# Attention outputs stored undivided, divided in the last unit and in the projection; row maxima made behind the values of a step

## The chip, the cores and the metric

The kernel runs on one core of a Trainium2 chip. The metric is the device time of one execution, in microseconds. A core has five engines that run side by side, each through its own instruction stream in order: TensorE (PE: matmuls; PEld is its weight load), VectorE (DVE), ScalarE (ACT), GpSimd (POOL) and SyncE (SP, which here only issues DMAs). Matmuls write to banks of PSUM; everything else lives in SBUF or in DRAM.

## The reference

One transformer block with conditioning, for `x` of 2 batches x 2048 tokens x 512 features, 16 heads of width 32:

```python
mod = silu(condition) @ Wada + bada
sh_a, sc_a, gt_a, sh_m, sc_m, gt_m = split(mod, 6)
xm = layernorm(x, g1, be1) * (1 + sc_a) + sh_a
q, k, v = split_heads(xm @ Wqkv)
attn = softmax(where(causal, q @ k.T / sqrt(32), -inf))
x = x + gt_a * ((attn @ v) @ Wproj + bproj)
xm = layernorm(x, g2, be2) * (1 + sc_m) + sh_m
x = x + gt_m * (gelu(xm @ W1 + b1) @ W2 + b2)
```

What the change is about is the division inside the softmax: `attn @ v` is the sum of `exp(score - max) * v` over the keys, divided by the sum of `exp(score - max)`.

## The kernel before

The program runs five stages one after the other: QKV of batch 0 (`Qkv.run`), attention of batch 0 (`attention_phase`), projection of batch 0 (`project_phase`) with QKV of batch 1 behind it, attention of batch 1, and projection of batch 1 with the MLP of both batches behind it.

**Units and steps.** Attention is cut into 16 units per batch. Unit `u` is a pair `(c, i)`: `c` is a chunk of four heads (128 features) and `i` a block of 512 queries (`QB`). The list is `units`: for `c` = 0 the blocks come as 0, 1, 2, 3, for `c` = 1, 2, 3 as 0, 2, 1, 3. A unit has `4i + 3` steps, each over one tile of 128 keys (`steps_of`): 3, 7, 11 or 15 steps. The four last units (12 to 15) belong to `c` = 3; their blocks are `last_order` = 0, 2, 1, 3, and the last unit is block 3 with 15 steps.

**A step.** `scores_t` puts on PE, for each of the four heads, a matmul that lays minus the row maxima into a bank (`st<-fold,sel`), then the scores with keys on the partitions on top of it (`st<-qst,kst`). ACT makes `e` = exp of the bank; on the diagonal POOL clears what is masked (`affine_select`). Two steps later (`LAG` = 2) PE multiplies `e` with the values into the PSUM bank `o` (`values`) and with ones into the bank `sm` (`row_sums`; off the diagonal POOL first adds two steps' `e` into `ee`, so that one matmul serves two steps). These late matmuls wait in the list `pending` and are put on PE by `flush(now)`, after the step's scores.

**The maxima.** The maxima must be known before a unit starts, so its scores are computed a first time with queries on the partitions: `Row.score` puts those matmuls (`s<-kst,qst`) in between those of a step, up to two units ahead (`AHEAD`), at a pace that `due` works out. They go into the pool `ps_s`, which has two banks (one in a step may borrow an `st` bank instead). DVE reads each bank once for its maximum (`mx<-s`, line 363; with the causal mask, line 358) and so frees it. When a unit's maxima are complete, `split` makes two small copies (`mhl`) and `Row.rows` transposes them on PE into a bank of `ps_s` (`ps_m`) and spreads them on DVE into `fold`, one `fold` for even and one for odd units. In a step of `attention_phase`, `row.rows(u + 1)` stands between the scores and `flush(now)`.

**The end of a unit.** `finish` copies `o` and `sm` to SBUF on ACT (`ot`, `sums`). Then SP, DVE, SP, SP, DVE and SP take turns: a DMA spreads the sums over the partitions (`r<-sums`), DVE inverts them (line 532), a DMA writes them to DRAM (`r<-r`), a DMA reads them back, each row spread over 32 partitions (`rb<-r`), DVE multiplies (`ot<-ot,rb`, line 540), and a DMA stores the block (`o<-ot`) to `od[b][i][:, c, :]`.

**Projection.** `project_phase` takes the blocks in the order of `last_order`, four tiles of 128 tokens each: PE multiplies the loaded block (`at`) with `wproj` in four matmuls, DVE adds `x` (to which POOL has added `bgate`) and takes the statistics for the next norm. `wproj` and `bgate` are `Wproj` and `bproj` times the gate; `gate_weights` makes them in the QKV stage of the batch, with one matmul (`ps_rows`) and five DVE products. `Row.prefetch`, called in the last unit's step 3, loads the first two blocks (`at_s`), the first tokens (`xt_s`) and the next stage's first tokens (`next_s`) into the space of the keys `kst0`, which are no longer needed by then.

**Order.** PE's matmuls and ACT's exps and copies stay in the order in which the code issues them (`tc.keep_in_program_order`). What goes to DVE, POOL and the DMA queues is put in order by the framework's scheduler when the program is built; on the chip each engine then takes its stream strictly in that order, and waits at the first instruction that isn't ready. Tiles of one tag share a ring of `bufs` buffers: `qst` (the queries of a unit, 4 buffers), `kst0`, `e`, `ee`, and the PSUM banks.

Of the kernel before, what the change touches and what calls it, by code (L numbers as in the profile page):

```python
# [27 lines left out]
def dit_block_kernel(  # L28
# [94 lines left out]
    for r in (0, HD):  # L123
# [19 lines left out]
    wproj = bp.tile([P, C, D], F32, tag="wproj", name="wproj")  # L143
# [15 lines left out]
    ]  # L159
    rd = [  # L160
        [dram.tile([HC, QB], F32, tag=f"r{b}{u}", name=f"r{b}{u}") for u in range(C * NQ)]
# [44 lines left out]
    def rows_of(psum, r, b):  # L206

        ps = psum.tile([P, D], F32, tag="mm", name="ps_rows")
        g = slice(r * HD, (r + 1) * HD)
        mm(ps, pick[g, b, :], modr[g, :], start=True, stop=True)  # L210
        return ps
# [57 lines left out]
    class Row:  # L269
# [42 lines left out]

        def prefetch(self):

            st = bp.tile([P, HC, T], F32R, tag="kst0", name="kst")
            st = st.bitcast(F32).rearrange("p h t -> p (h t)")  # L320
            self.at_s = [
                st[:, n * C * QB : (n + 1) * C * QB].rearrange("p (c q) -> p c q", c=C)
                for n in range(2)
            ]
            self.xt_s = [st[:, (2 * C + n) * QB : (2 * C + n + 1) * QB] for n in range(TQ)]
            self.next_s = [
                st[:, (3 * C + n) * QB : (3 * C + n + 1) * QB] for n in range(TQ)
            ]
            b = self.b
            nc.sync.dma_start(self.at_s[0], od[b][last_order[0]])  # L330
            for t in range(TQ):
                nc.sync.dma_start(self.xt_s[t], x_rows(b * NT + last_order[0] * TQ + t))
            for t in range(TQ):
                if b + 1 < B:
                    nc.sync.dma_start(self.next_s[t], x_rows((b + 1) * NT + t))
                else:
                    nc.sync.dma_start(self.next_s[t], x1d[t])
            nc.sync.dma_start(self.at_s[1], od[b][last_order[1]])

# [97 lines left out]
    def attention_phase(row):  # L437
        b, vv, kst, qst = row.b, row.vv, row.kst, row.qst
        with pool(f"att{b}") as ap, pool(
# [77 lines left out]
            def finish(u, o, sm):  # L517

                c, i = units[u]
                ot = ap.tile([P, QB], F32, tag="ot", name="ot", bufs=3)
                act(nc.scalar.copy(ot, o))
                sums = ap.tile([P, QB], F32, tag="sums", name="sums", bufs=2)
                act(nc.scalar.copy(sums, sm))
                r = ap.tile([P, QB // HD], F32, tag="r", name="r", bufs=2)
                nc.sync.dma_start(
                    r, sums[0:P:HD, :].rearrange("h (p q) -> h p q", p=HD)  # L530
                )
                nc.vector.reciprocal(r, r)
                nc.sync.dma_start(
                    rd[b][u].rearrange("h (p q) -> (h p) q", p=HD), r
                )
                rb = ap.tile([P, QB], F32, tag="rb", name="rb")
                nc.sync.dma_start(
                    rb, rd[b][u].unsqueeze(1).to_broadcast([HC, HD, QB])
                )
                nc.vector.tensor_tensor(ot, ot, rb, ALU.mult)  # L540
                nc.sync.dma_start(od[b][i][:, c, :], ot)
# [33 lines left out]
            for u, (c, i) in enumerate(units):  # L575
# [5 lines left out]
                for n_step, tiles in enumerate(steps_of[u]):  # L581
# [8 lines left out]
                    es = scores_t(u, n_step, n)  # L590
                    if u + 1 < len(units) and row.rows_made == u + 1:
                        if last:
                            row.score(row.count(cum[-1], u + 1))
                        if last or (ready > u + 1 and n_step >= 1):
                            row.rows(u + 1)
                    if u == len(units) - 1 and n_step == 3:
                        row.prefetch()
                    flush(now)

# [217 lines left out]
    def gate_weights(psum, b):  # L817

        nc.sync.dma_start(wproj, Wproj.rearrange("(c p) f -> p c f", p=P))
        nc.sync.dma_start(bgate, bproj.partition_broadcast(P))  # L820
        ps = rows_of(psum, 0, b)
        nc.vector.tensor_tensor(bgate, bgate, ps, ALU.mult)
        for c in range(C):
            nc.vector.tensor_tensor(wproj[:, c, :], wproj[:, c, :], ps, ALU.mult)

    def project_phase(row, psum, between):
# [5 lines left out]
        with pool(f"proj{b}") as pp:  # L832
            n = 0
            ats = list(row.at_s)
            for k, i in enumerate(last_order):
# [6 lines left out]
                for t in range(TQ):  # L842
                    nt = b * NT + i * TQ + t
# [7 lines left out]
                    for c in range(C):  # L851
                        mm(
                            ps, at[:, c, t * P : (t + 1) * P], wproj[:, c, :],
                            start=(c == 0), stop=(c == C - 1),
                        )
                    nc.vector.tensor_tensor(xt, ps, xt, ALU.add)
                    stats(pp, xt, nt, mv2)
                    nc.sync.dma_start(x1d[nt], xt)
                    between(n)
# [5 lines left out]
    with pool("wada") as wp, pool("qkv0") as qp, pool(  # L865
# [86 lines left out]
        def also(g, n):  # L952
# [6 lines left out]
            elif g == 2 and n == 3:  # L959
                modulation(3)  # L960
                scale_shift(a2, c2, r_g2, r_be2, 3, 4)
            elif g == 2 and n == 5:
                gate_weights(ps_mm, 0)
# [8 lines left out]
    with pool("qkv1") as qp, pool("ps_qkv1", bufs=6, space=PSUM) as ps_mm:  # L972
# [11 lines left out]
        def also(g, n):  # L984
            if g == 1 and n == 5:
                gate_weights(ps_mm, 1)
# [360 lines left out]
```

## Time and profile before

| | us |
|---|---|
| median of 3 runs | 2585.14 (2582.82 to 2586.33) |
| the profiled execution, its own time | 2578.87 |
| its span, first to last instruction | 2577.2 |
| PE busy | 2502.1 (97%) |
| DVE busy | 1303.3 (51%) |
| ACT busy | 894.7 (35%) |
| POOL busy | 840.3 (33%) |
| granted TensorE clock, mean | 0.993 |

All stages lie in one span: attention of batch 0 runs from about 226 to 838 us, its projection to 896, QKV of batch 1 to 1097, attention of batch 1 to 1708, its projection to 1767, and the MLP to the end.

How to read it: a group's line gives the instructions, their summed busy time and the mean of one in ns, and behind the bar the idle time of that engine right before them with what ended it. A line of the table of waits gives the waiting instruction, the one it waited for, the summed time in us, how often, and the longest. In a timeline each line has start and length in us, the engine, the line of the kernel, the operation, what it writes from what it reads, and in brackets the idle time of that engine before it with what ended it. SPq is the queue of SP, whose entries show a DMA's issue, not its landing.

### The profile page before, as it was taken

The page shows a single profiled execution, that of the slowest core. Times are in us where ns is not written, and L with a number is a line of the kernel's source. Part 1 is how long each engine was busy: PE and PEld are TensorE (multiplying, and loading weights), DVE is VectorE, ACT ScalarE, POOL GpSimd, SP SyncE. Part 2 cuts the span into 40 slices and gives each one's busy share as a digit, 9 for nine tenths or more (in the row PEclk, how much of TensorE's full clock was granted, in tenths as well). Part 3 has the DMA queues.
Part 4 walks back from the last instruction along what each step waited for, and adds up shares of the span by engine and source line. Part 5 has one row for each costly group of instructions (what it writes and reads, how often), then busy time and mean ns, then how long its engine had stood idle before and what let it go on. Part 6 is the DMA issues. An engine that isn't in the chain of part 4 may idle for free.

```text
span 2577.2 us, 31684 instructions
## 1 busy us (share of the span) xinstructions
PE 2502.1 (97%) x11361; PEld 1184.8 (46%) x11361; DVE 1303.3 (51%) x2768; ACT 894.7 (35%) x1667; POOL 840.3 (33%) x1038
## 2 busy tenths in 40 slices
PE   7999999999999999999999999999999999999998
PEld 3444444444444444544444444444444444444443
DVE  3465657657560625656565665426343344434424
ACT  1213454544445011154545444533312311311310
POOL 0001454544546266245445455543100200100100
PEclk9999999999999999999999999999999999999999
DMA  6735123242210698641422212035223332332322
GB/s 217 225 118 147 40 53 73 60 87 71 60 35 32 237 290 290 206 86 55 87 71 61 60 55 83 34 102 173 90 94 110 106 102 77 132 102 76 137 82 94
DMA packets 137991, 277.62 MB, mean 108 GB/s; under 512 B 19509, under 2 KB 48221, under 8 KB 133738
## 3 DMA queue, kind: packets, MB, share of 16 engines
q1 hardware_dynamic: 132354, 252.49, 32.8%
q0 software_dynamic: 5376, 23.07, 2.5%
q8 instruction: 89, 1.46, 0.2%
q14 instruction: 68, 0.56, 0.1%
q10 hardware_dynamic: 104, 0.05, 0.0%
HBM read 201.64 MB, written 73.66 MB: 107 GB/s over the span
## 4 chain that ended last, share of the span: by engine, by line
PE 89%; DVE 5%; DMA 4%; issue 1%; ACT 1%; SPq 0%; POOL 0%; DVEq 0%; ACTq 0%; POOLq 0%
PE st L187 18%; PE ps_h L187 15%; PE ps_y L187 15%; PE o L187 9%; PE s L187 8%; PE ps_qk L187 8%; PE sm L187 6%; PE ps_v L187 4%; PE ps_o L187 3%; DMA rb<-r 2%; DVE mx L363 2%; DVE junk L358 1%; PE ps_xt L195 1%; DMA r<-r 1%; DMA x<-in_x_dram 0%
## 5 line engine op out<-in xcount | busy, mean ns | idle before, releaser
L482 ACT ACTIVATE e<-st 128x512 f32<-128x512 f32 (+1 forms) x1152 | 575.6, 576 | 569.8 <-PE st L187 532.2
L507 POOL TENSOR_TENSOR ee<-e 128x512 f32<-128x512 f32 x384 | 485.0, 1292 | 442.1 <-ACT e L482 266.8
L363 DVE TENSOR_REDUCE mx<-s 128x1 f32<-128x512 f32 x616 | 414.0, 686 | 284.3 <-PE s L187 283.3
L187 PE MATMUL s<-kst,qst 128*128 128x512 f32 (+3 forms) x1058 | 451.6, 446 | 18.5 <-DVE mx L358 9.6
L187 PE MATMUL st<-qst,kst 128*128 128x512 f32 (+3 forms) x1280 | 435.9, 390 | 0.0
L187 PE MATMUL o<-e,vv 128*32 128x512 f32 (+3 forms) x2560 | 293.1, 539 | 0.0
L358 DVE CUSTOM_DVE_ANT_0 junk<-s,causal 128x384 bf16<-128x384 f32 (+3 forms) x442 | 211.3, 478 | 152.4 <-PE s L187 144.5
L187 PE MATMUL ps_h<-sx,w 128*128 128x512 f32 x640 | 286.7, 592 | 0.0
L187 PE MATMUL ps_y<-sh,w 128*128 128x512 f32 x640 | 276.6, 592 | 0.0
L187 PEld LDWEIGHTS st<-qst,kst 128*128 128x128 f32 x1280 | 227.8, 189 | 87.5 <-issue 63.0
L187 PEld LDWEIGHTS s<-kst,qst 128*128 128x128 f32 x1058 | 198.6, 189 | 150.3 <-DVE mx L363 54.4
L487 POOL TENSOR_SCALAR_AFFINE_SELECT e<-e 128x128 f32<-128x128 f32 (+1 forms) x384 | 125.2, 333 | 402.8 <-ACT e L482 395.8
L187 PE MATMUL ps_qk<-xmT,wqkv 128*128 128x512 f32 x512 | 243.9, 604 | 2.2 <-DVE xmT L243 2.2
L1118 POOL TENSOR_TENSOR c<-c 128x512 f32<-128x512 f32 x32 | 40.6, 1269 | 616.0 <-DVE c L1080 584.4
L1080 DVE TENSOR_TENSOR h<-c,ps_h 128x512 f32<-128x512 f32 x128 | 88.0, 688 | 231.4 <-PE ps_h L187 231.3
L187 PEld LDWEIGHTS ps_h<-sx,w 128*128 128x128 f32 x640 | 121.1, 190 | 150.2 <-issue 149.7
L187 PEld LDWEIGHTS ps_y<-sh,w 128*128 128x128 f32 x640 | 120.7, 190 | 147.8 <-issue 146.4
L187 PE MATMUL st<-fold,sel 32*128 32x512 f32 (+1 forms) x1152 | 164.4, 485 | 2.6 <-DVE mhl L378 2.2
L187 PEld LDWEIGHTS st<-fold,sel 32*128 32x128 f32 x1152 | 66.0, 183 | 197.1 <-ACT e L482 107.5
L1104 ACT ACTIVATE h<-h,cols 128x512 f32<-128x512 f32 x128 | 92.4, 722 | 181.9 <-DVE h L1080 181.9
L187 PEld LDWEIGHTS ps_qk<-xmT,wqkv 128*128 128x128 f32 x512 | 95.6, 193 | 100.6 <-issue 93.2
L187 PE MATMUL ps_v<-wqkv,xmT 128*128 128x512 f32 x256 | 122.7, 595 | 2.1 <-ACT xmT L248 2.1
(119 smaller groups left out, 2256.7 us busy)
## 6 DMA issues: line engine op xcount, KB each, us to landing
qst<-q SPq DMA_DIRECT2D x128, 256.0 KB
w<-w1d SPq DMA_DIRECT2D x34, 896.0 KB
w<-w2d SPq DMA_DIRECT2D x28, 1024.0 KB
kst<-k SPq DMA_DIRECT2D x24, 1024.0 KB
q<-hl SPq DMA_DIRECT2D x32, 512.0 KB
k<-hl SPq DMA_DIRECT2D x32, 512.0 KB
kst<-k SPq DMA_DIRECT2D x32, 256.0 KB
rb<-r SPq DMA_DIRECT2D x32, 256.0 KB
```

What stands on the lines that cost most here:

```text
L187: return tc.keep_in_program_order(nc.tensor.matmul(*args, **kw))
L195: return tc.keep_in_program_order(nc.tensor.transpose(dst, src, ident[:n, :n]))
L358: nc.vector.tensor_tensor_reduce(junk[:, :w], s[:, :w], causal[:, QB - w :], 1.0, MASKED, ALU.add, ALU.max, m,)
L363: nc.vector.tensor_reduce(m, s[:, :w], axis=AX.X, op=ALU.max)
L482: act(nc.scalar.activation(e[:, :w], sts[h][:, :w], AF.Exp))
L487: nc.gpsimd.affine_select(d, d, pattern=[[0, len(tiles)], [1, P]], compare_op=ALU.is_ge, fill=0.0, base=0, channel_multiplier=-1,)
L507: nc.gpsimd.tensor_tensor(out[h], es0[h], es1[h], ALU.add)
L1080: nc.vector.tensor_tensor(dst, x, y, op)
L1104: nc.scalar.activation(d, d, AF.Gelu, bias=col(r_b1 + chunk, 1))
L1118: nc.gpsimd.tensor_tensor(c1_, c1_, c2_, ALU.subtract)
```

## The change

- `finish` stores `ot` undivided (into the same `od`), and the four rows of sums of the unit as they are into a new DRAM tile `sd[b][i]` that collects the four chunks of a block. The inverse, its two DMAs and the product `ot<-ot,rb` leave it.
- The division moves to where a block is loaded. `Row.inverses` loads the sums of a whole block (2048 queries-and-heads x 4 chunks spread as 128 x 64), inverts them on DVE, writes them to `rd[b][i]` and reads them back spread over 32 partitions, one DMA for each chunk. `prefetch` does this for the first two blocks, with one product of 128 x 2048 for each (`kst<-kst,qst`); `project_phase` does it for the other two, issuing from ACT's queue (`nc.scalar`), with four products of 128 x 512 for each (`at<-at,qst` and `at<-at,rb`). The spread inverses of three of the blocks, and `next_s`, use buffers of the ring `qst`.
- `wproj` moves into the space of `kst0`, and `gate_weights` from the QKV stage into the last unit's step 7 (its loads into `prefetch`).
- `row.rows(u + 1)` is put after `flush(now)`: the transposition of the maxima stands behind the values and sums of the step instead of ahead of them.

```diff
@@ -140,7 +140,6 @@
     mv2 = const.tile([P, B * NT, 2], F32, tag="mv2", name="mv2")
     rstd2 = const.tile([P, B * NT], F32, tag="rstd2", name="rstd2")
 
-    wproj = bp.tile([P, C, D], F32, tag="wproj", name="wproj")
     bgate = bp.tile([P, D], F32, tag="bgate", name="bgate")
     n_cond = B * C
     r_g1 = n_cond
@@ -157,8 +156,12 @@
         [dram.tile([2, P, T], F32, tag=f"k{b}{c}", name=f"k{b}{c}") for c in range(C)]
         for b in range(B)
     ]
+    sd = [
+        [dram.tile([C, HC, QB], F32, tag=f"s{b}{i}", name=f"s{b}{i}") for i in range(NQ)]
+        for b in range(B)
+    ]
     rd = [
-        [dram.tile([HC, QB], F32, tag=f"r{b}{u}", name=f"r{b}{u}") for u in range(C * NQ)]
+        [dram.tile([C, HC, QB], F32, tag=f"r{b}{i}", name=f"r{b}{i}") for i in range(NQ)]
         for b in range(B)
     ]
     od = [
@@ -203,9 +206,9 @@
         nc.scalar.activation(rstd[:, lo:hi], mv[:, lo:hi, 1], AF.Sqrt, bias=eps)
         nc.vector.reciprocal(rstd[:, lo:hi], rstd[:, lo:hi])
 
-    def rows_of(psum, r, b):
-
-        ps = psum.tile([P, D], F32, tag="mm", name="ps_rows")
+    def rows_of(psum, r, b, tag):
+
+        ps = psum.tile([P, D], F32, tag=tag, name="ps_rows")
         g = slice(r * HD, (r + 1) * HD)
         mm(ps, pick[g, b, :], modr[g, :], start=True, stop=True)
         return ps
@@ -310,7 +313,33 @@
                 )
             self.qst[u] = t
 
+        def inverses(self, i, rb, queue):
+
+
+
+
+
+            sums, inv = [
+                d[self.b][i].rearrange("c h (p q) -> (c h p) q", p=P // (C * HC))
+                for d in (sd, rd)
+            ]
+            r = bp.tile([P, C * HC * QB // P], F32, tag="r", name="r", bufs=2)
+            queue.dma_start(r, sums)
+            nc.vector.reciprocal(r, r)
+            queue.dma_start(inv, r)
+            for c in range(C):
+                queue.dma_start(
+                    rb[:, c, :],
+                    rd[self.b][i][c].unsqueeze(1).to_broadcast([HC, HD, QB]),
+                )
+
+        def old_queries(self):
+
+            t = bp.tile([P, HC, QB], F32R, tag="qst", name="qst", bufs=AHEAD + 2)
+            return t.bitcast(F32)
+
         def prefetch(self):
+
 
 
 
@@ -323,10 +352,12 @@
                 for n in range(2)
             ]
             self.xt_s = [st[:, (2 * C + n) * QB : (2 * C + n + 1) * QB] for n in range(TQ)]
-            self.next_s = [
-                st[:, (3 * C + n) * QB : (3 * C + n + 1) * QB] for n in range(TQ)
-            ]
+            self.wproj = st[:, 3 * C * QB :].rearrange("p (c d) -> p c d", c=C)
+            t = self.old_queries()
+            self.next_s = [t[:, n, :] for n in range(TQ)]
             b = self.b
+            nc.sync.dma_start(self.wproj, Wproj.rearrange("(c p) f -> p c f", p=P))
+            nc.sync.dma_start(bgate, bproj.partition_broadcast(P))
             nc.sync.dma_start(self.at_s[0], od[b][last_order[0]])
             for t in range(TQ):
                 nc.sync.dma_start(self.xt_s[t], x_rows(b * NT + last_order[0] * TQ + t))
@@ -336,6 +367,19 @@
                 else:
                     nc.sync.dma_start(self.next_s[t], x1d[t])
             nc.sync.dma_start(self.at_s[1], od[b][last_order[1]])
+            for k in range(2):
+                rb = self.old_queries()
+                self.inverses(last_order[k], rb, nc.sync)
+                nc.vector.tensor_tensor(self.at_s[k], self.at_s[k], rb, ALU.mult)
+
+        def gate_weights(self):
+
+            ps = rows_of(ps_sp, 0, self.b, "s")
+            nc.vector.tensor_tensor(bgate, bgate, ps, ALU.mult)
+            for c in range(C):
+                nc.vector.tensor_tensor(
+                    self.wproj[:, c, :], self.wproj[:, c, :], ps, ALU.mult
+                )
 
         def width(self, u, h, t, kb):
             last = kb == units[u][1]
@@ -516,28 +560,12 @@
 
             def finish(u, o, sm):
 
-
-
-
-
                 c, i = units[u]
-                ot = ap.tile([P, QB], F32, tag="ot", name="ot", bufs=3)
+                ot = ap.tile([P, QB], F32, tag="ot", name="ot", bufs=2)
                 act(nc.scalar.copy(ot, o))
                 sums = ap.tile([P, QB], F32, tag="sums", name="sums", bufs=2)
                 act(nc.scalar.copy(sums, sm))
-                r = ap.tile([P, QB // HD], F32, tag="r", name="r", bufs=2)
-                nc.sync.dma_start(
-                    r, sums[0:P:HD, :].rearrange("h (p q) -> h p q", p=HD)
-                )
-                nc.vector.reciprocal(r, r)
-                nc.sync.dma_start(
-                    rd[b][u].rearrange("h (p q) -> (h p) q", p=HD), r
-                )
-                rb = ap.tile([P, QB], F32, tag="rb", name="rb")
-                nc.sync.dma_start(
-                    rb, rd[b][u].unsqueeze(1).to_broadcast([HC, HD, QB])
-                )
-                nc.vector.tensor_tensor(ot, ot, rb, ALU.mult)
+                nc.sync.dma_start(sd[b][i][c], sums[0:P:HD, :])
                 nc.sync.dma_start(od[b][i][:, c, :], ot)
 
 
@@ -588,14 +616,18 @@
                         due(u, starts[u] + n_step) - QB // 2, u + AHEAD
                     )
                     es = scores_t(u, n_step, n)
+                    make_rows = False
                     if u + 1 < len(units) and row.rows_made == u + 1:
                         if last:
                             row.score(row.count(cum[-1], u + 1))
-                        if last or (ready > u + 1 and n_step >= 1):
-                            row.rows(u + 1)
+                        make_rows = last or (ready > u + 1 and n_step >= 1)
                     if u == len(units) - 1 and n_step == 3:
                         row.prefetch()
+                    if u == len(units) - 1 and n_step == 7:
+                        row.gate_weights()
                     flush(now)
+                    if make_rows:
+                        row.rows(u + 1)
 
                     def tile_by_tile(dst, lhs, es, tiles, first, last):
                         at = 0
@@ -814,15 +846,6 @@
                     (w2d[:, f - FC // 2], w.rearrange("p n c d -> p n (c d)"))
                 )
 
-    def gate_weights(psum, b):
-
-        nc.sync.dma_start(wproj, Wproj.rearrange("(c p) f -> p c f", p=P))
-        nc.sync.dma_start(bgate, bproj.partition_broadcast(P))
-        ps = rows_of(psum, 0, b)
-        nc.vector.tensor_tensor(bgate, bgate, ps, ALU.mult)
-        for c in range(C):
-            nc.vector.tensor_tensor(wproj[:, c, :], wproj[:, c, :], ps, ALU.mult)
-
     def project_phase(row, psum, between):
 
 
@@ -832,6 +855,7 @@
         with pool(f"proj{b}") as pp:
             n = 0
             ats = list(row.at_s)
+            rbs = {}
             for k, i in enumerate(last_order):
                 if k in (0, 1):
 
@@ -840,6 +864,13 @@
                     ats.append(at)
                 at = ats[k]
                 for t in range(TQ):
+                    if n in (0, TQ - 1):
+                        d = 2 + n // (TQ - 1)
+                        rbs[d] = (
+                            row.old_queries() if d == 2
+                            else pp.tile([P, C, QB], F32, tag="rb", name="rb")
+                        )
+                        row.inverses(last_order[d], rbs[d], nc.scalar)
                     nt = b * NT + i * TQ + t
                     if k == 0:
                         xt = row.xt_s[t]
@@ -850,12 +881,15 @@
                     ps = psum.tile([P, D], F32, tag="mm", name="ps_o")
                     for c in range(C):
                         mm(
-                            ps, at[:, c, t * P : (t + 1) * P], wproj[:, c, :],
+                            ps, at[:, c, t * P : (t + 1) * P], row.wproj[:, c, :],
                             start=(c == 0), stop=(c == C - 1),
                         )
                     nc.vector.tensor_tensor(xt, ps, xt, ALU.add)
                     stats(pp, xt, nt, mv2)
                     nc.sync.dma_start(x1d[nt], xt)
+                    if k in (1, 2):
+                        d = ats[k + 1][:, t, :]
+                        nc.vector.tensor_tensor(d, d, rbs[k + 1][:, t, :], ALU.mult)
                     between(n)
                     n += 1
         inv_std(mv2, rstd2, b * NT, (b + 1) * NT)
@@ -959,8 +993,6 @@
             elif g == 2 and n == 3:
                 modulation(3)
                 scale_shift(a2, c2, r_g2, r_be2, 3, 4)
-            elif g == 2 and n == 5:
-                gate_weights(ps_mm, 0)
 
         with pool("hl0") as hp:
             qkv.run(hp, also)
@@ -982,8 +1014,6 @@
         project_phase(first, ps_mm, between)
 
         def also(g, n):
-            if g == 1 and n == 5:
-                gate_weights(ps_mm, 1)
             if n % 3 == 1:
                 quarters.step()
 
```

## The prediction

> **What bounds the kernel now.** The page's first part comes first: one engine is busy nearly all the time.
>
> ```profile
> PE 2502.1 (97%) x11361; PEld 1184.8 (46%) x11361; DVE 1303.3 (51%) x2768; ACT 894.7 (35%) x1667; POOL 840.3 (33%) x1038
> ```
>
> So PE sets the end, and 2577.2 - 2502.1 = 75 us is what it stood still. The second view is the table of PE's waits over the whole span; its largest rows are these:
>
> ```profile
> PE ps_m L195 <- DVE mx L358: 11.8, 18, 0.9
> PE s L187 <- DVE mx L358: 9.6, 7, 3.9
> PE s L187 <- DVE mx L363: 7.3, 7, 1.8
> PE ps_m L195 <- DVE mx L363: 5.7, 8, 0.8
> PE ps_m L195 <- DVE mhl L378: 3.0, 2, 1.5
> ```
>
> The reader is to see that half of the idle time hangs on DVE and is of two kinds. The transposition `ps_m` waits 28 times, 20.5 us in all. The maxima's matmul `s` waits 14 times, 16.9 us; the same table over the two attention stages alone (226 to 838 and 1096 to 1708 us) leaves 5.7 + 6.6 = 12.3 us for `s` in 11 waits, the rest lies in the QKV stages. Why `s` waits shows in the timeline, here at a place of unit 13:
>
> ```profile
> 710.60 0.87 DVE L540 TENSOR_TENSOR ot<-ot,rb 128x512 f32<-128x512 f32 x1 [1.86 <-ACT e L482]
> 711.39 0.68 DVE L363 TENSOR_REDUCE mx<-s 128x1 f32<-128x512 f32 x1
> 712.12 0.71 PE L187 MATMUL s<-kst,qst 128*128 128x256 f32 x2 [1.77 <-DVE mx L363]
> ```
>
> DVE stood 1.86 us in front of the product `ot<-ot,rb`, whose spread inverses hadn't landed (the label names an exp that the product doesn't read; at 19 of these products it names `rb<-r`, 37.5 us in all); the maxima behind it couldn't start, no bank of `ps_s` came free, and PE lost 1.77 us. I looked for such a product within 4 us ahead of each of the 11 waits, and found one each time. The `ps_m` waits look like this (end of unit 14's fifth step):
>
> ```profile
> 773.69 1.20 PE L187 MATMUL st<-qst,kst 128*128 128x512 f32 x4
> 776.36 0.33 PE L195 MATMUL ps_m<-ident,mhl 128*128 128x128 f32 x1 [1.48 <-DVE mhl L378]
> 776.62 1.07 PE L187 MATMUL sm<-ee,ones 128*32 128x512 f32 x8
> 777.50 1.04 PE L187 MATMUL o<-e,vv 128*32 128x512 f32 x8
> 778.47 0.51 PE L187 MATMUL st<-fold,sel 32*128 32x512 f32 x4
> ```
>
> PE waits 1.48 us for the last copies of the maxima, while 1.85 us of values and sums (776.62 to 778.47) that need nothing from DVE stand right behind it.
>
> [...]
>
> **The change part by part.** Where the edits land I took from the changed program's order of instructions on each engine.
>
> *Rows behind the values.* 28 of the 32 transpositions move (four, around the start of each batch's attention, have the same neighbours as before). Now the step's values and sums stand ahead of `ps_m`: 1.0 us where both are of 256 columns, 1.85 us at the wait of 1.48. That covers each wait, so 20.5 us go. None of the 28 is followed at once by a matmul on the `fold` it makes; that unit starts a step or more later. What is late next is its bank: `ps_m` holds one of two until `fold` (0.82) is written, about 1.2 us after PE reached it. In 22 cases PE spends that time on `st<-fold` (0.43), `st` (0.33) and the first `s` (0.23); in 6 (units 3, 7 and 11) an `s` follows directly and I charge 0.5 us each. Sum: -20.5 + 3.0 = **-17.5** (ends -22, as each wait also swallows the 0.16 us by which a matmul's record outlasts the next one's start, and 0, see the rivals).
>
> *Products leave units 0 to 13.* 28 products (0.69) and 28 inverses (0.25) leave DVE's stream, and with them the waits for landing: **-12.3** us of `s` waits (ends -16 and -8). Of each unit's three SP issues (`r<-sums`, `r<-r`, `rb<-r`) one is left, the store of the sums; nothing on PE waits for them.
>
> *The product for the first block.* It is 128 x 2048[...]. The scheduler puts it not in the last unit but in unit 14, behind the 625th of the batch's 640 maxima, the one at 760.46 here:
>
> ```profile
> 753.61 0.28 PE L187 MATMUL st<-qst,kst 128*128 128x256 f32 x1
> ...
> 760.46 0.69 DVE L363 TENSOR_REDUCE mx<-s 128x1 f32<-128x512 f32 x1
> 762.89 1.29 DVE L363 TENSOR_REDUCE mx<-s 128x1 f32<-128x512 f32 x2 [1.75 <-PE s L187]
> ```
>
> Its four spread loads (256 KB each, issued by SP) overwrite the queries of unit 13, so they start after that unit's last `st`, at 753.61 above: about 754.0. The time for four I take from three in a row:
>
> ```profile
> 440.16 0.42 SPq L305 DMA_DIRECT2D qst<-q  x1
> 441.24 0.54 SPq L537 DMA_DIRECT2D rb<-r  x1
> 441.83 0.47 SPq L305 DMA_DIRECT2D qst<-q  x1
> 447.45 0.69 DVE L540 TENSOR_TENSOR ot<-ot,rb 128x512 f32<-128x512 f32 x1 [1.63 <-issue]
> ```
>
> Three transfers of 256 KB took 447.45 - 440.16 = 7.3 us; with a fourth at a third more, 9.7. Landed at 763.7, product until 766.0, the next maximum until 766.7. PE needs that bank for its third `s` at 763.82, so it loses 2.9 us, twice: **+6**. At best the loads land before 761.1 and only the product counts (+1 in all); at worst they go one by one at the 6 us of the slowest single `rb` wait, 24 us less some overlap, say 770 (+12). Behind the product wait 15 maxima, and for them PE.
>
> *The other three blocks.* The second product and inverse lie behind the 640th maximum, where DVE idles 18 us (790s); the third and fourth lie in the projection, where DVE is busy 12 of 40 us: 8 x 0.69 = 5.5 us more, while 6 banks hold 6 x 3.43 us of PE's tiles (8 records at 13.73 us for 32 in the chain). Hidden, so 0; without that cover 5.5 us a batch. ACT gains 6 DMA issues among its exps and 6 behind them in each batch; SP's issues take 0.31 to 0.56 us, ACT idles 0.85 us or more in each of these steps, so I charge 0.5 a batch (0 to 2). The inverses' store there waits for DVE, long done: 0.
>
> *Gate weights.* Five products (3.4 us of DVE) leave the QKV stage, where they cost one `s` wait of 0.3 us at 153.5: **-0.3**. In the last unit DVE is free. POOL's four additions of `bgate` (1.28 each) now fall between two `ee` of a pair, 5.1 us into a stream that had 1.56 us of slack per pair and some 8 us (two and a half steps of 3.3) until the sums are due: I charge 0.5 a batch (0 to 3).
>
> *Projection of batch 0.* PE waits 0.91 + 0.66 = 1.6 us there for late `x` tiles, held up behind the last block's product. That chain is gone from DVE: **-1.6** (ends -2, +3, as the loads of weights, block and inverses now meet).
>
> Sum: -17.5 - 12.3 + 6 + 1 + 1 - 0.3 - 1.6 = **-23.7 us**. The profiled execution took 2578.87 (span 2577.2 and 1.7 around it), so it would be 2555.2; it ran 6.3 us under the median of the runs, 2585.14, on which I set the forecast: **2561 us**.
>
> **The rivals.**
> *The row's wait only moves* (faster, but little): the bank that `ps_m` holds is wanted at once, and PE waits behind it what it waited ahead of it. For it: two banks, and DVE at 64% (99.7 of 155 us from 440 to 595). Against: 22 of 28 have 1 us of other matmuls between. Then the 17.5 us are 0 and 2585 - 6 = 2579.
> *The spread inverses come late* (slower): one mechanism in one place, unit 14, with DVE in front of the 2048-wide product and 15 maxima, then PE, behind it. It decides from 2.9 + 12 = 15 us a batch, that is if the four loads took more than 21 us. The slowest single `rb` wait in the chain is 6.3 us, so four strictly one by one would do it: 754 + 25 + 2.3 + 0.7 = 782 against 763.8, 18 us a batch, and 2561 - 6 + 36 = 2591. Against it: the three that overlapped in 7.3 us.
> *Nothing*: the waits of `s` come back at other maxima because DVE as a whole is late; 2585. Against: DVE idles in every step (for instance 1.75 us at 762.89).
>
> **How the numbers follow.** The forecast has 0.76, the moved wait 0.12, the late inverses 0.06, nothing 0.06. A measurement here can tell about 0.2% (5.2 us) from no change. Faster: 0.76 and most of 0.12; same: the rest of that and most of nothing; slower: the late inverses and a little. The low end is -22 - 16 + 1 - 2 with the other costs at 0, about 2548; the high end takes in the moved wait, 2578.
>
> **What would show it.** Right: in the table of waits over the attention stages, `ps_m` under 4 us and `s` under 9; DVE's groups without `ot<-ot,rb`; the two 2048-wide products[...], the first after a wait of about 2.5 us, with one `s` wait of about 3 us in each unit 14. Wrong: `ps_m` gone but as much new time on `s` right after it; exps waiting behind ACT's DMAs; `sm<-ee` waiting for POOL in the last unit by over 2 us; a product of the first block that waits over 10 us.

## The result, and the profile after

The changed kernel took 2569.93 us (median of 4 runs, 2566.70 to 2571.46) against 2583.98 for the kernel before (4 runs, 2581.43 to 2586.33): a ratio of 0.9944, with a 95% interval of 0.9927 to 0.9961. The profiled execution took 2566.7 us with a span of 2564.6, which is 12.6 us under the span of before; the medians are 14.1 us apart. The forecast had -23.7. The engines' line on the page, and the rows of its waits that answer to those shown of before:

```profile
PE 2502.6 (98%) x11361; PEld 1185.5 (46%) x11361; DVE 1301.8 (51%) x2732; ACT 895.4 (35%) x1667; POOL 845.1 (33%) x1038
```
```profile
PE s L190 <- DVE mx L407: 12.9, 4, 5.9
...
PE ps_xt L198 <- DVE xn L227: 6.4, 3, 3.3
PE st L190 <- ACT e L526: 6.0, 12, 1.2
PE ps_xt L198 <- DVE xt L887: 4.8, 2, 3.2
```

No row of `ps_m` is left in the table. But this row of `s` still has 12.9 us, nearly all of it in two waits of 5.9, and three other rows are larger than before: they had 3.0, 2.3 and 0.9 us. So I cut the spans at the first matmul of a unit or a stage and took the differences (batch 0 and batch 1, us):

| stretch | before | after | rows_only | stores_only | late16 | late16_bgate | rows_no_product |
|---|---|---|---|---|---|---|---|
| QKV, batch 0 | 227.6 | 225.1 | 227.7 | 225.9 | 225.4 | 225.5 | 228.3 |
| units 0 to 13 | 529.3, 530.1 | 510.4, 509.6 | 533.9, 529.6 | 521.0, 520.0 | 510.8, 511.4 | 511.4, 510.9 | 507.9, 511.1 |
| unit 14 | 28.5, 28.6 | 34.6, 34.4 | 30.4, 26.9 | 34.7, 34.7 | 26.9, 26.9 | 26.9, 26.9 | 26.9, 26.9 |
| unit 15 | 52.0, 51.9 | 56.3, 56.6 | 52.0, 51.9 | 54.6, 54.9 | 57.8, 57.8 | 52.7, 52.7 | 52.0, 51.9 |
| projection | 58.8, 59.1 | 63.6, 66.2 | 58.8, 59.1 | 63.0, 67.7 | 57.9, 59.1 | 57.5, 59.1 | 56.8, 59.1 |
| QKV, batch 1 | 201.5 | 196.5 | 197.8 | 198.2 | 196.0 | 201.7 | 197.4 |
| MLP | 809.9 | 811.3 | 811.7 | 811.6 | 811.2 | 809.9 | 811.1 |

From before to after, units 0 to 13 gained 39.3 us, 9.5 more than the forecast's first two terms together, and the QKV stages 7.5. Unit 14 gave back 12.0, unit 15 9.0 and the projections 11.9; 1.3 lie in the MLP, which takes 809.9 to 811.7 us in all kernels of this study. The other columns belong to the experiments. Each column is one profiled execution, and the executions of one kernel differ: the profiled ones of rows_only, gate_only and pool_only took 5.8, 5.3 and 13.5 us more than the median of theirs, those of proj_pin and best 7.1 and 7.3 us less.

**Unit 14, the first block's product.** A timeline of after, DVE and PE at the place:

```profile
739.14 0.69 DVE L407 TENSOR_REDUCE mx<-s 128x1 f32<-128x512 f32 x1
745.62 2.31 DVE L373 TENSOR_TENSOR kst<-kst,qst 128x2048 f32<-128x2048 f32 x1 [5.80 <-DMA qst<-r]
747.85 1.27 DVE L407 TENSOR_REDUCE mx<-s 128x1 f32<-128x512 f32 x2
...
748.58 1.39 PE L190 MATMUL s<-kst,qst 128*128 128x512 f32 x2 [5.94 <-DVE mx L407]
```

The four spread loads were issued from 732.61 us on and landed at 745.62, 13.0 us later. DVE stood 5.80 us in front of the product, the maxima stood behind it, and PE waited 5.94. The scores of the next two maxima had been on PE at 741.12 and 741.59 us (0.39 us each); DVE took both at 747.85, after the product. Then PE ran slowly for a while. Three rows of the table by stretches (start and end, length, PE busy, granted clock, DMA share, GB/s) show that:

```profile
742.60:748.60 6.00, 0.06 (x2) 0.75 0.09 35
748.60:751.80 3.20, 3.20 (x22) 0.50 0.00 0
751.80:755.00 3.20, 3.20 (x21) 0.90 0.24 87
```

PE was granted 0.50 of its clock in the 3.2 us after the wait, and 0.90 in the next 3.2. The step cost 7.4 us for a wait of 5.9.

**Unit 15, POOL's additions.** The timeline of after, around the last pairs of `ee`:

```profile
797.26 5.02 POOL L880 TENSOR_TENSOR kst<-kst,bgate 128x512 f32<-128x512 f32 x4
802.25 4.95 POOL L551 TENSOR_TENSOR ee<-e 128x512 f32<-128x512 f32 x4
...
803.54 0.60 ACT L526 ACTIVATE e<-st 128x512 f32<-128x512 f32 x1 [1.43 <-POOL ee L551]
...
804.19 0.50 PE L190 MATMUL st<-fold,sel 32*128 32x512 f32 x1 [1.15 <-ACT e L526]
805.41 0.49 PE L190 MATMUL st<-fold,sel 32*128 32x512 f32 x1 [0.72 <-ACT e L526]
...
806.95 1.91 PE L190 MATMUL sm<-ee,ones 128*32 128x512 f32 x8
```

The chain runs through a buffer: `ee` is late, so the `e` that it reads isn't freed, the next exp has nowhere to write, the bank of `st` isn't freed, and PE waits 1.87 us. The eight sums behind it took 1.91 us, where the eight at 798.14 us took 1.06, and the granted clock was 0.53:

```profile
802.50:805.80 3.30, 1.43 (x8) 1.00 0.00 0
...
806.90:810.50 3.60, 3.60 (x18) 0.53 0.00 0
```

The step lost 3.9 us. From 802.50 to 805.80 us PE was busy for 1.43 of 3.3 us, where in unit 14 it was busy for 0.06 of the 6.0 us ahead of the low clock.

**Projection.** In batch 1 (DVE, then PE, of after) the spread inverses of the last block land one by one:

```profile
1704.29 0.69 DVE L892 TENSOR_TENSOR at<-at,rb 128x512 f32<-128x512 f32 x1 [4.24 <-DMA rb<-r]
1709.01 0.69 DVE L892 TENSOR_TENSOR at<-at,rb 128x512 f32<-128x512 f32 x1 [3.43 <-DMA rb<-r]
1712.88 0.69 DVE L892 TENSOR_TENSOR at<-at,rb 128x512 f32<-128x512 f32 x1 [2.57 <-DMA rb<-r]
1716.55 0.69 DVE L892 TENSOR_TENSOR at<-at,rb 128x512 f32<-128x512 f32 x1 [2.88 <-DMA rb<-r]
...
1721.48 1.76 PE L198 MATMUL ps_xt<-ident,xn 128*128 128x128 f32 x7 [3.25 <-DVE xn L227]
```

The scheduler had put these products ahead of work that PE waits for. In batch 0 the same loads hold ACT itself, whose queue issues them: the four issues took 6.58 us from 837.67 us on.

### The profile page after: what moved, and what is told of

The parts are those of the page before. It is cut to its first block, busy times and chain, and to the rows that moved or that the text cites. A ratio compares the mean times of both kernels' runs of the same rounds, so it can differ in the third digit from the quotient of the medians.

```text
span 2564.6 us, 31548 instructions
## 1 busy us (share of the span) xinstructions
PE 2502.6 (98%) x11361; PEld 1185.5 (46%) x11361; DVE 1301.8 (51%) x2732; ACT 895.4 (35%) x1667; POOL 845.1 (33%) x1038
## 4 chain that ended last, share of the span: by engine, by line
PE 91%; DMA 4%; DVE 2%; issue 1%; POOL 1%; ACT 1%; SPq 0%; ACTq 0%; DVEq 0%; POOLq 0%
PE st L190 20%; PE ps_y L190 15%; PE ps_h L190 15%; PE o L190 10%; PE s L190 9%; PE ps_qk L190 8%; PE sm L190 6%; PE ps_v L190 4%; PE ps_o L190 2%; DMA rb<-r 1%; PE ps_xt L198 1%; DMA qst<-r 1%; DVE mx L407 1%; POOL ee L551 1%; PE ps_o L198 0%
## 5 line engine op out<-in xcount | busy, mean ns | idle before, releaser
L526 ACT ACTIVATE e<-st 128x512 f32<-128x512 f32 (+1 forms) x1152 | 575.5, 576 | 556.7 <-PE st L190 511.1
L190 PE MATMUL s<-kst,qst 128*128 128x512 f32 (+3 forms) x1058 | 451.3, 446 | 15.7 <-DVE mx L407 12.9
L190 PEld LDWEIGHTS s<-kst,qst 128*128 128x128 f32 x1058 | 198.8, 189 | 140.5 <-DVE mx L407 57.5
```

Of the source, the lines that this page charges most:

```text
L190: return tc.keep_in_program_order(nc.tensor.matmul(*args, **kw))
L526: act(nc.scalar.activation(e[:, :w], sts[h][:, :w], AF.Exp))
```

## The experiments

Every ratio is against the kernel before on the same chip, with its 95% interval.

**rows_only.** The kernel before with `row.rows(u + 1)` behind `flush(now)`, nothing else.

```diff
+                    make_rows = False
...
-                        if last or (ready > u + 1 and n_step >= 1):
-                            row.rows(u + 1)
+                        make_rows = last or (ready > u + 1 and n_step >= 1)
...
                     flush(now)
+                    if make_rows:
+                        row.rows(u + 1)
```

> The kernel before with one edit, the row of the maxima behind the values and sums of the step. My theory (the 28 waits of ps_m go, 3.0 us come back as waits for a bank of ps_s): the term of the forecast was -17.5 us, up to -22 if each wait also swallows the tail of the record ahead of it, so 2562 to 2567 us against a before of 2584; ps_m below 4 us in the table of PE's waits, s at about the 16.9 us of before. Rival (the wait only moves to the next s behind the same bank): 2579 to 2584 and s at 30 us or more.

Measured: 0.9986 (0.9977 to 0.9995), 3.7 us. The `ps_m` waits did go (20.5 to 2.3), but `s` has more than in before, where it had 16.9:

```profile
PE s L187 <- DVE mx L363: 13.5, 11, 3.0
...
PE s L187 <- DVE mx L358: 7.2, 6, 2.3
...
PE ps_m L195 <- DVE mhl L378: 2.3, 1, 2.3
...
PE s L187 <- DVE fold L422: 2.1, 4, 0.5
```

My theory fell for this kernel: the time is near the rival's. The rival's mechanism is not what the trace shows, though: `s` waits 22.8 us, not 30, and only 2.1 us of them name the bank that `ps_m` holds (`fold`). Most hang on maxima; the steps that lost most against after are the second of units 6, 10, 11 and 13. At unit 11's DVE waits longer for the spread inverses than it did in before, and the maxima behind it are late. First rows_only:

```profile
632.68 1.56 DVE L540 TENSOR_TENSOR ot<-ot,rb 128x512 f32<-128x512 f32 x1 [2.91 <-DMA rb<-r]
```

and before:

```profile
633.01 0.69 DVE L540 TENSOR_TENSOR ot<-ot,rb 128x512 f32<-128x512 f32 x1 [1.39 <-DMA rb<-r]
```

The waits are only a part of it. In units 0 to 13 PE stood still for 26.5 us against 34.3 in before, but the same matmuls kept it busy for 1037.0 us against 1025.1, at a lower granted clock: 0.97 against 0.99 in batch 0, and in batch 1 0.97, 0.99 and 0.97 against 0.98, 1.00 and 0.99 (1100 to 1300, 1300 to 1500 and 1500 to 1630 us). The rows for batch 0, first before:

```profile
227.56:756.84 529.28, 512.64 (x3379) 0.99 0.28 68
```

and rows_only:

```profile
227.66:761.59 533.93, 519.70 (x3378) 0.97 0.28 67
```

At unit 11's second step, behind the wait above, the 512-wide matmuls take 0.63 us each instead of 0.39. How much of this the other executions of rows_only have is not shown; the profiled one is the second slowest of 19.

**rows_no_product.** rows_only without the product of `ot`.

```diff
-                nc.vector.tensor_tensor(ot, ot, rb, ALU.mult)
```

> The kernel before with the row of the maxima behind the values, and without the product of ot with the spread inverses (its output is not divided by the sums; the inverse and its three DMAs stay). With the product in place the moved row brought only 3.7 us. My theory (what the row no longer waits for, DVE waits for in front of that product: its inverses land a fixed time after a unit's end, and PE now comes sooner): without the product the 14 units before unit 14 take 510 to 513 us in each batch, as in the changed kernel, against 530 to 534 with it; in all 30 to 38 us under before, 2542 to 2550. Rival (ps_m holds a bank of ps_s, and s waits behind it): s keeps most of its 20 us of waits, the units stay above 520 us, 2560 or more.

Measured: 0.9803 (0.9785 to 0.9820), 2530.9 us, below even the expected 2542 to 2550. Units 0 to 13 took 507.9 and 511.1 us and no wait of `s` is left in the attention stages. So the moved row gains fully once no product waits in DVE's stream, and the mean granted clock of the profiled execution is 0.996, against 0.988 in that of rows_only. It is also a mark for the division: all that the changed kernel spends on it, and on the gate's move, is by the two ratios about 36 us over this one.

**stores_only.** The changed kernel with the row back ahead of `flush`.

```diff
-                        make_rows = last or (ready > u + 1 and n_step >= 1)
+                        if last or (ready > u + 1 and n_step >= 1):
+                            row.rows(u + 1)
...
                     flush(now)
-                    if make_rows:
-                        row.rows(u + 1)
```

> The changed kernel with the row of the maxima put back ahead of the values; everything else of the change stays. If the parts add up, it lies above the changed kernel (2570) by what the row brings, 17.5 to 22 us: 2587 to 2592, so the rest of the change would by itself be no gain at all; ps_m back at about 20 us, s in the attention stages only at the two products of the first block. Rival (the row brings little and the undivided stores bring the gain): 2572 to 2578.

Measured: 1.0043 (1.0026 to 1.0059), 2591.4 us, as expected; by the two ratios it lies 1.0% above after, some 25 us, a little over the expected 17.5 to 22. The row is worth 10.6 and 10.4 us in units 0 to 13 here (stores_only against after), and the stores 8.3 and 10.1 (before against stores_only). Alone one part gains 0.14% and the other loses 0.43%; together they gain 0.56%.

**gate_only.** The kernel before with `gate_weights` in the last unit's step 7 and its loads in `prefetch`.

```diff
                         row.prefetch()
+                    if u == len(units) - 1 and n_step == 7:
+                        row.gate_weights()
...
-                gate_weights(ps_mm, 0)
```

> The kernel before with one edit, the gate's products of wproj and bgate in the last unit's step 7 (loads in prefetch; wproj keeps its own buffer). My theory, from the two traces: the QKV stages gain 2.2 and 5.0 us (the 3.9 us wait of s near 955 us hung on a load of x behind the loads of wproj and bgate), and POOL's four additions of bgate fall between two pairs of ee and cost PE 3.9 us a batch: -7.2 + 7.8, so 2584 to 2586, and st<-fold waits for exps in unit 15 by about 1.9 us a batch. Rival (the additions are free, and the 3.9 us in the changed kernel come from ACT's DMA issues among its exps, which this kernel doesn't have): 2576 to 2578, and no such wait.

Measured: 1.0040 (1.0024 to 1.0056), a loss of 11 us where I had about none. Half of the theory holds: unit 15 grew to 56.3 and 57.6 us with the waits of `st<-fold` for exps and with no DMA on ACT, and QKV of batch 0 shrank by 2.6. The other half fell: QKV of batch 1 took 204.9 us instead of gaining 5.0. That stage stands at 196 to 198 us in some of these kernels and at 201 to 207 in others, with and without the gate in it. In the latter PE stands still longer there (7.3 to 12.4 us against 4.3 to 6.8), in waits of `s` for maxima. In before, with 201.5 us for the stage, a wait of 3.88 us that ends at 954.71 us is followed by a granted clock of 0.50 from 956 to 959 us; in after, with 196.5, the mean clock from 888 to 1088 us is 1.00. Why these maxima are late, no run here settles.

**bgate_dve.** The additions to the first tokens on DVE.

```diff
-                    nc.gpsimd.tensor_tensor(xt, xt, bgate, ALU.add)
+                    on = nc.vector if k == 0 else nc.gpsimd
+                    on.tensor_tensor(xt, xt, bgate, ALU.add)
```

> The changed kernel with one edit: the four additions of bgate to the first tokens go on DVE (idle in the last unit) instead of POOL. My theory (they stood 5.0 us in POOL's stream between two pairs of ee; exps then found no free buffer of e, and PE lost 3.9 us in step 10 of unit 15): 3.9 us a batch come back, about 7.8 us under the changed kernel, 0.991 to 0.992 of before; st<-fold no longer waits for an exp in unit 15. Rival (ACT's six DMA issues among the exps delay them): the wait stays and the time is that of the changed kernel, 0.994.

Measured: 0.9939 (0.9918 to 0.9961), not apart from after. In the trace the edit did what was expected: unit 15 fell from 56.3 and 56.6 to 52.7 and 53.1 us, and no wait of over 0.3 us for an exp is left. QKV of batch 1 was 201.8 us in this kernel instead of 196.5, and took 5.4 of the 7 us back.

**prod_late.** Both 128x2048 products behind the last `fold` on DVE.

```diff
-                nc.vector.tensor_tensor(self.at_s[k], self.at_s[k], rb, ALU.mult)
+                with tc.issue_after(self.last_fold.ins):
+                    nc.vector.tensor_tensor(self.at_s[k], self.at_s[k], rb, ALU.mult)
...
-            nc.vector.tensor_tensor(
+            self.last_fold = nc.vector.tensor_tensor(
```

> The changed kernel with one edit: both 128x2048 products are put behind the last fold on DVE, so the first one stands behind the 640th maximum instead of behind the 625th. My theory (the maxima and then PE stood behind a product whose four spread loads took 13 us): the 7.4 us that unit 14 lost in each batch come back, 2570 - 15 = 2555 us; no s wait of over 1 us in the attention stages. Rival (DVE as a whole is late there, so the next maxima are waited for anyway): 2565 to 2570.

Measured: 0.9895 (0.9879 to 0.9911), 2553.9 us. Unit 14 takes 26.9 us in both batches; the `s` wait is gone. The rival is out.

**proj_pin, pool_only.** Two edits of the projection: the last block's products pinned behind the statistics of the 8th to 11th tile, and its DMAs issued by POOL.

```diff
-                    if k in (1, 2):
-                        d = ats[k + 1][:, t, :]
-                        nc.vector.tensor_tensor(d, d, rbs[k + 1][:, t, :], ALU.mult)
+                    if 7 <= n < 11:
+                        d = ats[3][:, n - 7, :]
+                        tc.keep_in_program_order(
+                            nc.vector.tensor_tensor(d, d, rbs[3][:, n - 7, :], ALU.mult)
+                        )
+                    if k == 1:
+                        d = ats[2][:, t, :]
+                        nc.vector.tensor_tensor(d, d, rbs[2][:, t, :], ALU.mult)
```
```diff
-                        row.inverses(last_order[d], rbs[d], nc.scalar)
+                        row.inverses(
+                            last_order[d], rbs[d], nc.scalar if d == 2 else nc.gpsimd
+                        )
```

> The changed kernel with one edit: the four products of the last block in the projection stand behind the statistics of the 8th to 11th tile on DVE, instead of as early as the scheduler put them. My theory (there DVE stood 8.0 us for the load of the block in batch 0 and four times for a spread load, 13.1 us, in batch 1; the sums into xt behind it came late and PE had no bank): the projections shrink from 63.6 and 66.2 us to about 59.5 each, 11 us under the changed kernel, 0.990 of before; ps_xt waits for xt below 2 us in all. Rival (the loads of weights, blocks, tokens and inverses are late as a whole, whatever DVE's order): xt waits for its own load and the projections stay above 62 us.

> The changed kernel with one edit: the six DMAs of the last block's inverses are issued by POOL, which is idle there, instead of ACT. My theory for the projection of batch 0 (ACT stands in those issues until 844.3 us, its rstd comes behind them, DVE waits 6.2 us for rstd, the x1d store of the fourth tile and with it SP's loads of the last block and of the tokens come late, and then DVE stands 8.0 us for the block): that projection falls from 63.6 to 58 to 60 us; batch 1, which has no rstd there, keeps its 66 us; in all 2564 to 2566, 0.992 of before. Rival (the 3 MB of wqkv ahead of them in the DMA engines make these loads late): it keeps its 63 to 64 us.

Measured: proj_pin 0.9998 (0.9988 to 1.0009), slower than after: the projection of batch 0 grew to 71.2 us, with PE now waiting 4.8 us for `at` itself, and that of batch 1 shrank to 64.3 (3.0 us of such waits). Both stay above 62 us, as the rival had it. Order alone is not the cause; in batch 0 the operands are late: DVE waits 10.6 us there for a tile of tokens (`xt`), whose load POOL had waited for. pool_only 0.9918 (0.9885 to 0.9951): batch 0 fell to 61.2 us, half of what I expected, and batch 1 to 59.8, where I had expected nothing. What both batches share is the spread loads themselves, so the next run changes those.

**best, best_pool.** The three edits of prod_late, bgate_dve and proj_pin together, and the same with POOL as the queue.

> The changed kernel with three edits: both 128x2048 products behind the last fold, the additions of bgate on DVE, the products of the last block pinned in the projection. If the three losses are separate, they add: 15 + 8 + 11 = 34 us under the changed kernel, some 48 under before, 0.981 of it. If one wait hides another, less: 0.985.

> The kernel of the run best with the last block's inverses issued by POOL. If ACT's issues are what is late in the projection of batch 0, its 71.8 us fall below 62, and with batch 1 at 62 the whole is 10 us under best: 0.985 to 0.986 of before. If the transfers themselves are late, it stays at 0.989 to 0.990.

Measured: 0.9899 (0.9876 to 0.9922) and 0.9865 (0.9846 to 0.9884). best is no faster than prod_late alone: its projection of batch 0 took 71.8 us. best_pool came near the expected time, but not in the expected way: that projection fell to 65.3 us and not below 62, batch 1's to 59.1, and QKV of batch 1 took 207.2.

**late16.** prod_late with the spread cut by head instead of by chunk.

```diff
-            for c in range(C):
+            for h in range(HC):
                 queue.dma_start(
-                    rb[:, c, :],
-                    rd[self.b][i][c].unsqueeze(1).to_broadcast([HC, HD, QB]),
+                    rb[h * HD : (h + 1) * HD, :, :],
+                    rd[self.b][i][:, h].unsqueeze(0).to_broadcast([HD, C, QB]),
                 )
```

> prod_late with one edit: the inverses are spread by one DMA for each head (32 partitions from one source of 4 rows) instead of one for each chunk (4 heads x 32 partitions); the same four DMAs of 256 KB. In the changed kernel four of them, alone on the DMA engines, took 12 us at a busy share of 0.2 of 16 engines and about 100 GB/s. My theory[...]: with 32 outermost they run at 300 GB/s or more and land within 5 us. Rival (reading one row 32 times from DRAM is what is slow): again 12 us at 100 GB/s. As the products wait for nothing in unit 14 here, the time should stay at that of prod_late (0.9895 of before), less what the waits for rb in the projection give, up to 5 us.

Measured: 0.9848 (0.9834 to 0.9863), 2542.4 us; by the two ratios 12 us under prod_late, where I had allowed for 5. The DMA view of 730 to 748 us, in 40 slices: the busy share of the 16 DMA engines in tenths, and GB/s. First after:

```profile
DMA  0000000021222222222222224222222200000000
GB/s 0 0 0 0 0 0 0 0 18 41 86 100 100 109 100 100 105 96 109 100 100 109 91 109 137 100 109 96 105 105 96 105 32 9 0 0 0 0 0 18
```

and late16:

```profile
DMA  0000000002699999999640001000000000008710
GB/s 0 0 0 0 0 0 0 0 0 32 146 187 259 341 246 232 237 232 200 123 87 9 0 0 36 0 0 0 0 0 0 0 0 0 0 0 314 273 32 0
```

The same 1 MB takes 13 slices of 0.45 us instead of 26, 5.9 us instead of 11.7. With next to nothing else on the DMA engines (1.05 of the 1.07 MB in the 18 us of after are on the queue of these loads), the loads of after keep 2 tenths of the 16 busy, those of late16 up to 9 tenths. The rival is out, since each row is still read 32 times. What differs is the cut: by chunk the outermost dimension of what is read is 4 long, by head 32. How the cut comes to change the busy share was not shown. The 300 GB/s that I expected were reached in one slice only.

The projections fell to 57.9 and 59.1 us, from 63.0 and 66.6 in prod_late, which is where before stood. The view of the tile `rb` shows one reason (min, median and max of an issue in ns). First after:

```profile
L331 ACTq DMA_DIRECT2D rb<-r x8: 517/540/4886, 837.7 to 1697.9; - x8
```

and late16:

```profile
L331 ACTq DMA_DIRECT2D rb<-r x8: 309/404/486, 833.4 to 1690.2; - x8
```

In after one issue held ACT 4.9 us in batch 0. ACT's `rstd` stood behind it, DVE waited 6.2 us for that, and the loads of the last block and of the tokens went out late.

**late16_bgate.** late16 with the edit of bgate_dve.

> late16 with the four additions of bgate on DVE. If these additions in POOL's stream are what makes st<-fold wait 2.8 us for an exp in the last unit, unit 15 falls from 57.8 us to the 52.7 us that the other kernels with this edit have, 10 us in all: 2532 us, 0.981 of before. If ACT's DMA issues among its exps are what holds the exps (eight issues stand there instead of six), unit 15 stays above 56 us and the time at 2542.

Measured: 0.9846 (0.9832 to 0.9859), 2538.2 us. Unit 15 fell to 52.7 us as expected, so ACT's issues hold nothing there, but QKV of batch 1 took 201.7 us against 196.0. The ratio is not apart from that of late16. Both are faster than before by 1.5%, and by the two ratios than after by about 1.0%.

## Why the prediction was right, and where not

The direction and the range held; the size of most terms did not. By the stretches the gains came to 46.8 us against 31.7 forecast, the costs to 34.2 against 8. That both were too small and so cancelled in part is luck: the forecast gains with the measured costs would have left no gain at all. (The range's low end, by its own terms, is 2546 and not 2548.)

- **Rows behind the values, -17.5 forecast.** -21.0 measured with the stores in place, inside its ends: each wait went (18.0 us of `ps_m` in these units of stores_only), and the 3.0 us of banks were not paid. But I priced the term as if it stood alone. Alone it is -3.7; the rival "the row's wait only moves" has the right size for that kernel, if not the right cause, and is wrong for the whole change. The failed step is the addition of the first two terms: as long as `ot<-ot,rb` waits in DVE's stream, what was freed in front of `ps_m` is spent on maxima behind that product and on matmuls at a lower granted clock (0.97 against 0.99 in batch 0).
- **Products leave units 0 to 13, -12.3 forecast.** -18.4 by stores_only, outside my ends of -16 and -8. I counted the waits only, and these were sized well: PE stands still for 22.5 us there instead of 34.3. The other 6.6 us are busy time of PE, for the same matmuls; what they are, no run here shows.
- **First block's product, +6 forecast.** +14.9 (7.44 and 7.42), outside my ends. The product took 2.31 us, as the forecast's 763.7 to 766.0 has it. The trace of before gives that price too: its products have medians of 693 ns for 512 columns (`ot<-ot,rb`) and 1225 for 1024 (`sh<-h,h`), and a straight line through the two is at 2.29 us for 2048, an estimate. The landing was not right. I took 9.7 us for four loads from "three transfers in 7.3 us", but those three were a spread load between two loads of queries, and there the DMA engines were busy for 0.45 of the time (440.0 to 447.5 us) instead of 0.24 (734.0 to 745.7 us of after). The four took 13.0. And 5.9 us of wait cost 7.4, as said above.
- **ACT's issues and POOL's additions, +2 forecast.** +9.0 in unit 15. The pair of `ps_rows` matmuls, which moved there from the QKV stage, adds 1.05 us in step 7, of which 0.6 come back in step 8. The additions cost 3.9 a batch, against 0.5 and an end of 3 (2.3 to 5.5 in the other kernels traced with them in this place). The slack of "two and a half steps" was that of the sums; the buffers of `e`, which `ee` frees, have less. ACT's issues among the exps cost nothing that shows: with them unit 15 took 52.7 us in late16_bgate, against 52.0 and 51.9 in before, and 0.45 of that is the pair's.
- **Other three blocks hidden, 0; projection of batch 0, -1.6.** +4.7 and +7.1. The second product was hidden in unit 15 as said. For the other two I had compared DVE's work with its idle time. The work did fit. Its operands didn't come in time, and DVE, which takes its stream in order, stood 2.57 to 4.24 us in front of each of the last four products in batch 1.
- **QKV, -0.3 forecast.** -2.5 in batch 0, where 1.1 to 3.4 us are gained in each kernel with the gate moved. The -5.0 in batch 1 are not shown to be the gate's: rows_only, which leaves the gate where it was, has 3.7 of them.
- Of what would show it right: `ps_m` under 4 held; `s` under 9 did not (12.1 in the attention stages, both large waits at the first product, each twice what was expected). Of what would show it wrong: POOL's lateness came, by way of `e` rather than `sm<-ee`.

The slower rival had the right mechanism, spread inverses late in unit 14, at half its size: 7.4 us a batch against the 15 from which it decides.

## What to carry to other kernels

A product that waits for a transfer belongs in an engine's stream only where nothing urgent is behind it (in unit 14 the 5.80 us of DVE cost PE 5.94); ask of each such instruction when its operand lands, not whether the engine has time. Before taking a transfer's time from another one's, look at the share of the DMA engines that the two keep busy (0.45 and 0.24 here): the cut by head instead of by chunk was alone worth a factor of two here, 5.9 us against 11.7. Two edits that free the same engine's waits are not added; each is priced with the other in place.

## What the runs showed of the hardware that I had not expected

- In two places a wait of PE cost more than its length: 5.9 us of idleness were followed by 3.2 us at a granted clock of 0.50, and 1.9 us of idleness in two pieces by 3.6 us at 0.53.
- Loads issued by ACT can hold ACT: four issues of 0.54 us in the median took 6.6 us in the projection of batch 0, one of them 4.9, while 3 MB of weights were being loaded.
